# Four graph layers on one core: finer waits on reused memory, and a symmetry proof moved and split

## The chip, the cores and the metric

The kernel runs on one core of a Trainium2 chip. The metric is the device time of one execution in microseconds. The core has five engines with instruction streams of their own: TensorE (PE, with PEld for its weight loads), VectorE (DVE), ScalarE (ACT), GpSimd (POOL) and SyncE (SP). SP, ACT and POOL issue DMA transfers. Each engine takes its instructions in the order in which the program's scheduler put them.

## The reference

`x` is 4096 x 128 and `adj` is 4096 x 4096, symmetric, of zeros and ones with ones on the diagonal. Four layers follow each other, each `x = layernorm(x + layer(x, adj))`:

```python
# layer 0: hyperbolic attention; h from x @ weight.T on the Poincare ball
adj_att = adj * sigmoid((x_tangent @ wl)[:, None] + (x_tangent @ wr)[None, :] + att_b)
support = einsum('ij,ijd->id', adj_att, logmap(h_i, h_j));  out = proj(expmap0(proj(expmap(h, support))))
# layer 1: four heads of 32; masked softmax of q k^T by adj, gated skip connection
# layer 2: relu(D^-1/2 (adj + I) D^-1/2 x @ weight)
# layer 3: H = x W^T + b; softmax over leaky_relu(s_i + r_j) where adj > 0, times H
```

## The kernel before

The program holds two versions. `Fast` runs always; it uses that `adj` is symmetric and of two values, and it collects marks in `odd` that are not zero if this is false. At the end a flag made of the marks decides whether the general version, `Net`, runs the whole again. For these inputs it doesn't. Everything below is about `Fast`.

Rows are cut into 8 stripes of 512 (`NS` = 8, `S` = 512), so `adj` is 8 x 8 blocks of 512 x 512, each held as [128 partitions, 4, 512].

*Layer 0, prologue* (`layer0`, to about 75 us): x is loaded, turned (`HT`), multiplied by the weight, and scaled on the ball (`HA`, lines 446 to 453). PSUM is `ps_t` with 6 banks and `ps_c` with one. Two adjacency blocks (`early`) are loaded ahead.

*Layer 0, pair loop* (`pair_loop`, to 643 us): over the 36 pairs (I, J) with I <= J, each loading one f32 block (`ad`) and doing both sides of the pair. The order of its instructions is written out by hand (`SHARED_ORDER`, `manual_schedule`). Beside it, `narrow` has POOL's queue copy `adj` to a bf16 version in DRAM, `adjb`.

*Proof and tail* (643 to 742 us): `mirror` proves that `adj` is symmetric. For each of the 28 pairs I < J it fetches both blocks of `adjb` (`low`, `up`, SP's queue, three of each in flight), for the 8 diagonal blocks one. TensorE adds, into one PSUM bank `pm`, minus `low` (line 1699) and plus `up` turned (line 1704), with the factor 2^k in the k-th of 12 blocks (`sized`), so that any difference is left as a nonzero number; VectorE reduces each full bank to a mark (line 1709). In the same time the layer's tail on VectorE and ScalarE (lines 533 to 602 and `normalise_tile`) makes the new X, group by group of four tiles.

*Layer 1, prologue* (`layer1`, 742 to 790 us): X is turned into `XT` (line 166), the q and k projections are cut into two parts (`cut`, lines 2217 to 2221), stored to DRAM (`qk`), and fetched back stacked by POOL's queue (`stack`, line 2195) into `KS` and `QS`; then `V` (in `VA`) and `R` (in `Y`). `attention_unshifted` follows, again in a hand-written order: 8 row stripes, each of 32 steps with scores (`ps`, line 2007), exponential (line 2014), mask (line 2016) and sums (`pv`, line 2033). It also copies `adj` into blocks of f32 in DRAM, `adjf`.

*Layers 2 and 3* (`layers23`, from 1603 us): blocks of `adjf` run through a ring of 8 slots in SBUF (`ring`, loads at line 2337), are multiplied by `Y` in two parts (`halves`, lines 2362 to 2382), and looked at for values other than 0 and 1 (line 2346). Small weights (`w`, `br`, `wn`, `ac`) are loaded by SP's queue ahead of the ring's loads. `attend_factored` is layer 3.

Memory comes from tile pools, opened and closed like a stack. In the kernel before, a new pool that lies over the memory of a closed one waits until all of the closed pool's tiles are done with. Outside the hand-written stretches the scheduler orders each engine's instructions by readiness and priority (earlier in the program is higher).

Of the kernel before, what the change touches and what calls it, by code (L numbers as in the profile page):

```python
# [9 lines left out]
F32 = mybir.dt.float32  # L10
# [7 lines left out]
P = 128  # L18
# [7 lines left out]
S = 512  # L26
# [35 lines left out]
class Net:  # L62
# [30 lines left out]

    def copies(self):
        self.adjT = self.dram.tile([self.NS, self.NS, P, 4, S], F32, tag="adjT", name="adjT")

    def pools(self, ctx, adj, big, t, o):

        self.on_scalar = 4
        if adj:  # L100
            self.adjp = ctx.enter_context(self.tc.tile_pool(name="adjp", bufs=adj))
        if big:
            self.ps_big = ctx.enter_context(self.tc.tile_pool(name="ps_big", bufs=big, space=PSUM))
        self.ps_t = ctx.enter_context(self.tc.tile_pool(name="ps_t", bufs=t, space=PSUM))
        self.ps_o = ctx.enter_context(self.tc.tile_pool(name="ps_o", bufs=o, space=PSUM))
# [4 lines left out]
    def whole(self, I, J):  # L110
        return self.adjT[I, J]

# [19 lines left out]
    def load_row(self, vec, name, pool=None):  # L132

        t = (pool or self.const).tile([P, vec.shape[0]], F32, tag=name, name=name)
        self.nc.sync.dma_start(out=t, in_=vec.partition_broadcast(P))
        return t
# [7 lines left out]
    def load_mat(self, mat, name, pool=None):  # L144
        t = (pool or self.const).tile(list(mat.shape), F32, tag=name, name=name)
        self.nc.sync.dma_start(out=t, in_=mat)
# [164 lines left out]
    def layer0(self, x, weight, bias, att_w, att_b):  # L311
# [4 lines left out]
        with ExitStack() as ctx:  # L316
            self.on_scalar = 4
            keep = ctx.enter_context(tc.tile_pool(name="keep0", bufs=1))
            self.cols = ctx.enter_context(tc.tile_pool(name="cols0", bufs=1))
            adp = ctx.enter_context(tc.tile_pool(name="ad0", bufs=2))  # L320
            pre_pools = ctx.enter_context(ExitStack())
            pre = pre_pools.enter_context(tc.tile_pool(name="pre0", bufs=2))
            self.ps_t = pre_pools.enter_context(tc.tile_pool(name="ps_t", bufs=6, space=PSUM))
            one = pre_pools.enter_context(tc.tile_pool(name="one0", bufs=1))
            self.wide = pre_pools.enter_context(tc.tile_pool(name="wide", bufs=1))
            ps_c = pre_pools.enter_context(tc.tile_pool(name="ps_c", bufs=1, space=PSUM))
# [14 lines left out]
            early = {p: self.load_block(adp, 0, p) for p in range(2)}  # L341

# [171 lines left out]
            late = ctx.enter_context(tc.tile_pool(name="late0", bufs=1))  # L514
            rot = ctx.enter_context(tc.tile_pool(name="rot0", bufs=6))
# [92 lines left out]
    def pair_loop(self, HT, HA, dr, rows, adp, early, rows4):  # L608
# [7 lines left out]
        with ExitStack() as ctx:  # L616
            atp = ctx.enter_context(tc.tile_pool(name="at0", bufs=2))
            wtp = ctx.enter_context(tc.tile_pool(name="sg0", bufs=6))
            wk = ctx.enter_context(tc.tile_pool(name="wk0", bufs=2))
            ps_t = ctx.enter_context(tc.tile_pool(name="ps_t0", bufs=2, space=PSUM))  # L620
            ps_z = ctx.enter_context(tc.tile_pool(name="ps_z0", bufs=2, space=PSUM))
            ps_i = ctx.enter_context(tc.tile_pool(name="ps_i0", bufs=1, space=PSUM))
            ps_j = ctx.enter_context(tc.tile_pool(name="ps_j0", bufs=1, space=PSUM))
# [224 lines left out]
    def layer1(self, Wq, bq, Wk, bk, Wv, bv, Ws, bs, Wb, R):  # L848
# [6 lines left out]
        with ExitStack() as ctx:  # L855
            self.on_scalar = 4
            keep = ctx.enter_context(tc.tile_pool(name="keep1", bufs=1))
# [27 lines left out]
            with ExitStack() as pctx:  # L885
                pre = pctx.enter_context(tc.tile_pool(name="pre1", bufs=1))
                rot = pctx.enter_context(tc.tile_pool(name="rot1", bufs=2))
                self.ps_t = pctx.enter_context(tc.tile_pool(name="ps_t", bufs=8, space=PSUM))
# [59 lines left out]
    def attention_unshifted(self, VA, KS, QS, at0, stack, R, wb):  # L948
# [4 lines left out]
        with ExitStack() as ctx:  # L953
            rot = ctx.enter_context(tc.tile_pool(name="rotf", bufs=1))
            natp = ctx.enter_context(tc.tile_pool(name="natf", bufs=2))
            atp = ctx.enter_context(tc.tile_pool(name="atf", bufs=1))
            ep = ctx.enter_context(tc.tile_pool(name="ef", bufs=3))
            ps_s = ctx.enter_context(tc.tile_pool(name="ps_s", bufs=3, space=PSUM))
            ps_v = ctx.enter_context(tc.tile_pool(name="ps_v", bufs=1, space=PSUM))
# [198 lines left out]
    def attention_shifted(self, V, qk, R, wb, spare):  # L1158
# [4 lines left out]
        with ExitStack() as ctx:  # L1163
            self.pools(ctx, 1, 2, 3, 1)
            self.wide = ctx.enter_context(tc.tile_pool(name="wide", bufs=2))
            keep = ctx.enter_context(tc.tile_pool(name="keeps", bufs=1))
            self.cols = ctx.enter_context(tc.tile_pool(name="cols1", bufs=1))
# [12 lines left out]
            work = ctx.enter_context(tc.tile_pool(name="work1", bufs=1))  # L1180
# [98 lines left out]
    def layers23(self, w2, weight, bias, a_s, a_r, out, Y):  # L1279
# [6 lines left out]
        with ExitStack() as ctx:  # L1286
            RING = 8
            ring = ctx.enter_context(tc.tile_pool(name="ring", bufs=1)).tile([P, RING, 4, S], F32, tag="ring", name="ring")
            keep = ctx.enter_context(tc.tile_pool(name="keep3", bufs=1))
# [10 lines left out]
            pre = pctx.enter_context(tc.tile_pool(name="pre3", bufs=1))  # L1300
            rot = pctx.enter_context(tc.tile_pool(name="rot2", bufs=2))
            wp = pctx.enter_context(tc.tile_pool(name="w2", bufs=4))
            ps_b = pctx.enter_context(tc.tile_pool(name="ps_b", bufs=2, space=PSUM))
# [342 lines left out]

class Fast(Net):

    MARKS = 160

# [934 lines left out]
```

## Time and profile before

| What | us |
|---|---|
| time, median of 3 runs (lowest, highest) | 2021.89 (2018.53, 2024.26) |
| time of the profiled execution | 2022.37 |
| its span, first to last instruction | 2020.6 |
| layer 0 prologue, to the first pair's matmul (L1782) | 75.5 |
| last ScalarE instruction of layer 0's tail (L235) ends | 717.3 |
| last mark of the proof (L1709) ends | 742.4 |
| first exponential of attention (L2014) | 790.4 |
| last sums of attention (L2033) end | 1587.5 |
| first ring matmul of layer 2 (L2382) | 1603.4 |

Busy over the whole span: PE 92%, DVE 86%, ACT 65%, POOL 8%. Lines of the profile name the engine, the line of the kernel, the tiles written and read, and durations; a wait `A <- B: t, n, m` says that A stood t us in all, n times, m at the longest, until B was done. In tables by stage each engine has its busy time and the number of its instructions; the columns after the engines are the granted TensorE clock as a share of full speed, the busy share of the DMA engines, and GB/s.

### The profile page before, as it was taken

What the parts mean: (1) busy time and instruction counts of PE and PEld (TensorE: products, weight loads), DVE (VectorE), ACT (ScalarE), POOL (GpSimd) and SP (SyncE); (2) the same over time, 40 slices, a digit from 0 to 9 for tenths busy, and PEclk for the clock granted to TensorE, in tenths of its full rate; (3) what the DMA queues carried; (4) which work ended last, traced back from release to release, by engine and by line L of the source; (5) the groups of instructions that cost most, each with busy time, mean ns of one, the idle gap of its engine ahead of it and who ended that gap; (6) DMA issues with size and microseconds to landing.
All of it is one profiled execution on the core that took longest, in us unless ns stands there. A gap on an engine that the chain in (4) does not pass through costs nothing.

```text
span 2020.6 us, 23440 instructions
## 1 busy us (share of the span) xinstructions
PE 1861.8 (92%) x8406; PEld 997.6 (49%) x8420; DVE 1738.0 (86%) x2741; ACT 1319.2 (65%) x1665; POOL 171.7 (8%) x269
## 2 busy tenths in 40 slices
PE   4789999999998677999999999999999798899997
PEld 4257776667667455333333333333333476644443
DVE  6579999898898846789998999999999888888986
ACT  5589999999997733777878787777877422210000
POOL 2212111121100311200000000000000000000000
PEclk8569999899998997999999999999999899999999
DMA  3488999898934978996767676768656699978882
GB/s 102 49 141 142 156 151 169 144 177 147 156 111 168 373 263 284 259 267 217 236 215 236 211 230 208 239 215 240 211 209 240 238 422 420 421 281 321 295 278 84
DMA packets 167247, 450.86 MB, mean 223 GB/s; under 512 B 13708, under 2 KB 56876, under 8 KB 142544
## 3 DMA queue, kind: packets, MB, share of 16 engines
q1 hardware_dynamic: 112128, 330.94, 45.3%
q0 software_dynamic: 45632, 50.69, 19.8%
q10 hardware_dynamic: 9360, 67.64, 10.4%
q8 instruction: 68, 1.11, 0.2%
q14 instruction: 59, 0.48, 0.1%
HBM read 472.20 MB, written 111.23 MB: 289 GB/s over the span
## 4 chain that ended last, share of the span: by engine, by line
PE 44%; DVE 25%; ACT 15%; DMA 11%; issue 5%; SPq 0%; ACTq 0%; POOL 0%; DVEq 0%; POOLq 0%
PE pv L2033 11%; PE pa L1576 10%; DVE e L2016 9%; PE ps L2007 6%; ACT e L2014 4%; DMA ring<-adjf 4%; PE pz L1782 4%; DMA up<-adjb 3%; PE pi L1866 2%; DVE nat L1998 2%; PE pj L1881 2%; ACT w L1799 2%; ACT s L1822 2%; PE pz L1785 2%; ACT y L1818 1%
## 5 line engine op out<-in xcount | busy, mean ns | idle before, releaser
L2016 DVE SCALAR_TENSOR_TENSOR e<-at,e 128x2048 f32<-128x2048 bf16 x256 | 582.7, 2286 | 78.4 <-ACT e L2014 77.8
L2014 ACT ACTIVATE e<-ps 128x1024 f32<-128x1024 f32 x512 | 493.1, 1024 | 150.0 <-PE ps L2007 122.0
L2033 PE MATMUL pv<-e,VA 128*64 128x512 f32 x2048 | 497.5, 607 | 6.4 <-DVE e L2016 6.1
L2007 PE MATMUL ps<-QS,KS 128*128 128x512 f32 x1024 | 314.4, 425 | 11.1 <-ACT e L2014 10.4
L2007 PEld LDWEIGHTS ps<-QS,KS 128*128 128x128 f32 x1024 | 170.5, 188 | 238.5 <-ACT e L2014 180.2
L2033 PEld LDWEIGHTS pv<-e,VA 128*64 128x64 f32 x2048 | 124.8, 136 | 250.2 <-issue 214.1
L1576 PE MATMUL pa<-w,Y 128*128 128x512 f32 x448 | 195.3, 594 | 0.0
L1782 PE MATMUL pz<-HT 128*128 128x512 f32 x288 | 173.5, 687 | 10.2 <-DVE w L1854 9.1
L1573 DVE SCALAR_TENSOR_TENSOR w<-rho,col,ring 128x512 f32<-128x512 f32 x224 | 162.8, 747 | 22.3 <-PE pa L1576 9.7
L1866 PE MATMUL pi<-HA,w 128*128 128x129 f32 x1152 | 157.5, 286 | 7.3 <-ACT s L1822 5.3
L1866 PEld LDWEIGHTS pi<-HA,w 128*128 128x128 f32 x1152 | 144.0, 199 | 19.1 <-issue 9.3
L2382 PE MATMUL pa<-ring,Y 128*128 128x512 f32 x512 | 133.1, 411 | 11.9 <-DVE ring L2357 10.0
L1576 PEld LDWEIGHTS pa<-w,Y 128*128 128x128 f32 x448 | 83.7, 190 | 106.1 <-issue 79.9
L1989 ACT ACTIVATE nat<-nat 128x2048 f32<-128x2048 f32 x64 | 122.5, 1915 | 4.1 <-DMA nat<-in_adj_dram 4.1
L1791 DVE TENSOR_SCALAR t<-pz 128x512 f32<-128x512 f32 x144 | 93.7, 684 | 30.3 <-PE pz L1785 30.3
L1881 PE MATMUL pj<-HA,w 128*128 128x129 f32 x896 | 117.5, 288 | 2.1 <-DVE X L1895 1.8
L2382 PEld LDWEIGHTS pa<-ring,Y 128*128 128x128 f32 x512 | 95.9, 192 | 42.3 <-DVE ring L2357 12.8
L1881 PEld LDWEIGHTS pj<-HA,w 128*128 128x128 f32 x896 | 109.9, 200 | 9.9 <-issue 7.2
L1854 DVE TENSOR_TENSOR w<-w,ptz 128x512 f32<-128x512 f32 x112 | 73.7, 681 | 23.5 <-PE ptz L1849 23.3
L1799 ACT ACTIVATE w<-di,dr 128x512 f32<-128x512 f32 x144 | 90.6, 708 | 1.9 <-DMA di<-rows 1.9
L2346 DVE SCALAR_TENSOR_TENSOR odd<-ring 128x1024 bf16<-128x1024 f32 x64 | 78.1, 1220 | 12.8 <-DMA ring<-adjf 12.3
L1830 DVE SCALAR_TENSOR_TENSOR t<-t,s 128x2048 f32<-128x2048 f32 x36 | 82.3, 2285 | 6.7 <-ACT s L1822 6.7
(410 smaller groups left out, 2338.5 us busy)
## 6 DMA issues: line engine op xcount, KB each, us to landing
ring<-adjf SPq DMA_DIRECT2D x128, 1024.0 KB, 12.9
nat<-in_adj_dram ACTq DMA_DIRECT2D x64, 1024.0 KB, 6.0
adjf<-in_adj_dram SPq DMA_DIRECT2D x64, 1024.0 KB, 7.4
ad<-in_adj_dram SPq DMA_DIRECT2D x36, 1024.0 KB, 9.2
adjb<-in_adj_dram POOLq DMA_DIRECT2D x64, 512.0 KB, 11.5
at<-adjb SPq DMA_DIRECT2D x63, 512.0 KB, 3.5
low<-adjb SPq DMA_DIRECT2D x36, 512.0 KB, 5.5
up<-adjb SPq DMA_DIRECT2D x28, 512.0 KB, 6.7
```

The costliest lines, as they stand in the source:

```text
L1573: nc.vector.scalar_tensor_tensor(w, rho[:, I * S : (I + 1) * S], col[:, 0, j : j + 1], at[:, jb, :], op0=ALU.max, op1=ALU.mult)
L1576: nc.tensor.matmul(pa, lhsT=F[:, j, :], rhs=w, start=False, stop=(j == NT - 1), skip_group_check=True)
L1782: nc.tensor.matmul(pz, lhsT=HT[:, j * P : (j + 1) * P], rhs=HT[:, I * S : (I + 1) * S], start=True, stop=False)
L1799: nc.scalar.activation(w[:, jb, :], st[p]["d"][k], AF.Sigmoid, bias=dr[:, 4 * J + jb : 4 * J + jb + 1])
L1866: nc.tensor.matmul(row[I, "po"][ib // 2][:, ib % 2, :], lhsT=st[p]["w0"][:, jb, ib * P : (ib + 1) * P], rhs=HA[:, 4 * J + jb, :], start=False,
L1881: nc.tensor.matmul(pj[:, a, :], lhsT=st[p]["w1"][:, ib, jb * P : (jb + 1) * P], rhs=HA[:, 4 * I + ib, :], start=(ib == 0), stop=(ib == 3),)
L1989: nc.scalar.activation(nat, nat, AF.Identity, accum_out=self.deg2[:, k, i : i + 1])
L2007: nc.tensor.matmul(p[:, h, :], lhsT=KS[:, h2 + h, jb * P : (jb + 1) * P], rhs=QS[I % 2][:, h2 + h, :], start=True, stop=True,)
L2014: nc.scalar.activation(e[:, h2 : h2 + 2, :], p, AF.Exp)
L2016: nc.vector.scalar_tensor_tensor(e, at[:, jb % 4, :].unsqueeze(1).to_broadcast([P, NH, S]), 0.0, e, op0=ALU.not_equal, op1=ALU.mult,)
L2033: nc.tensor.matmul(st["po"][h // 2][g : g + 64, :], lhsT=VA[:, o : o + 64], rhs=e[:, h, :], start=(jb == 0), stop=(jb == NT - 1), skip_gro ...
L2382: nc.tensor.matmul(st["pa"], lhsT=halves[k][:, j, :], rhs=at[:, jb, :], start=(I > 0 and j == k == 0), stop=(j == NT - 1 and k == 1), skip ...
```

## The change

`Fast` opens its pools with `reuse_waits="tile"`: a tile that is placed over memory of closed pools waits for the tiles that lay there, no longer for whole pools. `Net` keeps the waits by pool (`waits = "pool"`, `banks = 6`; in `Fast` they are "tile" and 5, and `EARLY` = 8).

The proof becomes `compare(ctx, pairs, natural)` and is split. Its first 8 pairs are compared in layer 0's prologue (`ahead`), from f32 blocks of `adj` itself, whose upper halves are read as bf16 with a step of two elements; their banks are reduced by a ScalarE square with a sum. The rest of the prologue is given higher priority than this comparison. PSUM there: `ps_t` 5 banks, `ps_c` one, the proof two. The other 20 pairs and the diagonal stay behind the pair loop, in pools at the other end of the memory (`side="right"`). These stay open while layer 1's prologue runs, which is given higher priority than they have; its `ps_t` falls from 8 banks to 6 and its `cut` buffers from 7 to 5. The scale tiles take 6 VectorE instructions where they took 25.

In `layers23` the two `halves` get a pool right behind the ring, and the small weights are loaded by POOL's queue.

```diff
+    waits = "pool"
+    banks = 6
+    def pool(self, **kw):
+        return self.tc.tile_pool(reuse_waits=self.waits, **kw)
...
-            keep = ctx.enter_context(tc.tile_pool(name="keep0", bufs=1))
+            keep = ctx.enter_context(self.pool(name="keep0", bufs=1))
...
-            self.ps_t = pre_pools.enter_context(tc.tile_pool(name="ps_t", bufs=6, space=PSUM))
+            self.ps_t = pre_pools.enter_context(self.pool(name="ps_t", bufs=self.banks, space=PSUM))
...
             early = {p: self.load_block(adp, 0, p) for p in range(2)}
+            self.ahead(pre_pools)
...
+    def ahead(self, ctx):
+        rank = self.tc.cur_priority
+        pairs = [(I, J) for I in range(self.NS) for J in range(I + 1, self.NS)][: self.EARLY]
+        self.compare(ctx, pairs, True)
+        ctx.enter_context(self.tc.high_priority(self.tc.cur_priority - rank + 1))
+
     def mirror(self, ctx):
+        NS = self.NS
+        self.proof, self.rank = ExitStack(), self.tc.cur_priority
+        pairs = [(I, J) for I in range(NS) for J in range(I + 1, NS)][self.EARLY :] + [(I, I) for I in range(NS)]
+        self.compare(self.proof, pairs, False)
+
+    def compare(self, ctx, pairs, natural):
+        keep = ctx.enter_context(self.pool(name="mir", bufs=1, side="right"))
+        rot = ctx.enter_context(self.pool(name="mirt", bufs=3, side="right"))
+        ps = ctx.enter_context(self.pool(name="mirp", bufs=2, space=PSUM, side="right"))
...
-        for k in range(K):
-            for m in range(2):
-                nc.vector.tensor_scalar(sized[:, m, k, :], eye, float((-1) ** m * 2**k), None, op0=ALU.mult)
+        nc.vector.tensor_copy(sized[:, 0, 0, :], self.ident)
+        for lo, n, by in ((1, 1, 2.0), (2, 2, 4.0), (4, 4, 16.0), (8, 4, 256.0)):
+            nc.vector.tensor_scalar(sized[:, 0, lo : lo + n, :], sized[:, 0, 0:n, :], by, None, op0=ALU.mult)
+        nc.vector.tensor_scalar(sized[:, 1, :, :], sized[:, 0, :, :], -1.0, None, op0=ALU.mult)
...
+        def fetch(tag, I, J):
+            if natural:
+                t = rot.tile([P, 4, S], F32, tag=tag, name=tag)
+                nc.sync.dma_start(
+                    out=t, in_=self.adj[J * S : (J + 1) * S, I * S : (I + 1) * S].rearrange("(a p) c -> p a c", p=P)
+                )
+                return t.bitcast(BF16)[:, :, 1 : 2 * S : 2]
+            t = rot.tile([P, 4, S], BF16, tag=tag, name=tag)
+            nc.sync.dma_start(out=t, in_=self.adjb[I, J])
+            return t
...
-            if last:
+            if last and natural:
+                nc.scalar.activation(p, p, AF.Square, accum_out=self.mark())
+            elif last:
                 nc.vector.tensor_reduce(self.mark(), p, AX.X, ALU.max, apply_absolute_value=True)
...
             with ExitStack() as pctx:
+                pctx.enter_context(self.proof)
+                pctx.enter_context(tc.high_priority(tc.cur_priority - self.rank + 1))
...
-                self.ps_t = pctx.enter_context(tc.tile_pool(name="ps_t", bufs=8, space=PSUM))
+                self.ps_t = pctx.enter_context(self.pool(name="ps_t", bufs=6, space=PSUM))
...
-                        cut = rot.tile([P, 2, S], F32R, tag="cut", name="cut", bufs=7)
+                        cut = rot.tile([P, 2, S], F32R, tag="cut", name="cut", bufs=5)
...
+            halved = ctx.enter_context(self.pool(name="halved", bufs=1))
+            halves = [halved.tile([P, NT, D], F32R, tag=f"Y{k}", name=f"Y{k}") for k in range(2)]
...
-            halves = [pre.tile([P, NT, D], F32R, tag=f"Y{k}", name=f"Y{k}") for k in range(2)]
...
-            w = self.load_mat(w2, "w2")
-            br = self.load_row(bias, "br3", keep)
-            wn = self.load_mat(weight, "wn3", pre)
+            w = self.load_mat(w2, "w2", queue=nc.gpsimd)
+            br = self.load_row(bias, "br3", keep, nc.gpsimd)
+            wn = self.load_mat(weight, "wn3", pre, nc.gpsimd)
...
-                nc.sync.dma_start(out=ac[:, k : k + 1], in_=v.unsqueeze(1))
+                nc.gpsimd.dma_start(out=ac[:, k : k + 1], in_=v.unsqueeze(1))
```

## The prediction

> **What bounds the kernel now.** I read the slices of the page first, for stages in which no engine is full; then busy time by stage at the places that the change touches; then the waits and the chain there. In the long loops TensorE, VectorE and ScalarE are all near full, so time can only come from the seams between stages. The change touches three: the first layer's prologue (0 to 75.5 us), the step from layer 0 to layer 1 (643 to 790), and the step from attention to layer 2 (1581 to 1603).
>
> Busy time of each engine by stage (length, then PE, PEld, DVE, ACT, POOL; granted clock, DMA share, GB/s):
>
> ```profile
> 31.00:46.00 15.00, 0.00 (x0) 0.00 (x0) 13.67 (x77) 10.07 (x17) 1.04 (x1) 0.53 0.00 1
> 46.00:68.00 22.00, 11.97 (x32) 5.85 (x32) 21.26 (x49) 11.34 (x32) 8.27 (x8) 0.50 0.00 0
> 75.50:108.50 33.00, 32.96 (x37) 9.65 (x38) 9.85 (x13) 22.40 (x15) 6.33 (x10) 0.50 0.62 76
> ...
> 694.00:717.50 23.50, 15.84 (x158) 9.99 (x160) 21.05 (x126) 14.05 (x40) 0.00 (x0) 1.00 0.99 367
> 717.50:742.40 24.90, 17.68 (x190) 12.47 (x191) 2.77 (x4) 0.00 (x0) 0.57 (x1) 1.00 0.74 256
> 742.40:786.00 43.60, 38.65 (x194) 29.49 (x194) 33.43 (x55) 13.05 (x20) 14.02 (x21) 0.84 0.96 322
> ...
> 1581.00:1587.60 6.60, 5.57 (x26) 1.59 (x26) 5.17 (x5) 2.82 (x6) 0.00 (x0) 1.00 0.00 0
> 1587.60:1603.00 15.40, 2.74 (x15) 2.11 (x14) 12.97 (x64) 4.07 (x10) 0.00 (x0) 0.64 0.71 280
> 1603.00:1760.00 157.00, 144.03 (x619) 109.42 (x619) 134.59 (x373) 37.29 (x118) 0.00 (x0) 0.98 1.01 417
> ```
>
> The prologue is VectorE's from 31 to 68 us; the DMA engines do nothing, and TensorE idles at half clock. From 717.5 to 742.4 VectorE works 2.8 us and ScalarE not at all. Layer 2 is bound by its transfers: DMA share 1.01 at 417 GB/s.
>
> The chain of waits through the second seam, and the waits at the second and third:
>
> ```profile
> 719.04 6.28 DMA up<-adjb
> ...
> 734.53 4.50 DMA low<-adjb
> ...
> 742.50 3.69 PE pt L166 x32
> ```
>
> ```profile
> POOL VA L2204 <- PE pm L1704: 54.3, 1, 54.3
> ACT XT L181 <- PE pt L166: 27.6, 1, 27.6
> ```
>
> ```profile
> SPq L2337 <- PE pv L2033: 13.4, 1, 13.4
> ...
> SPq L135 <- DVE X L2107: 10.7, 1, 10.7
> ```
>
> The mirror proof's fetches (low, up) run to 742; layer 0's last ScalarE instruction ends at 717.3. Layer 1's transposes (pt L166) start only when the proof has released its pools. At the third seam the ring's first loads (L2337) wait for the last pv matmul, and the queue then stands behind br (L135), which waits for attention's last normalisation.
>
> **The change, part by part.** (1) *Eight pairs leave the proof after the pair loop.* Its 28 pairs run from the first fetch at 642.9 to 726.9, 3.0 us each (1 MB at 350 GB/s), and its 8 diagonal blocks to 741.4. With 20 pairs the same pace ends at 642.9 + 60 + 14.5 = 717.4, just when the tail ends. That alone is 24 us. The scale tiles there, 24 instructions in 2.46 us before, become 6 over the same columns: 0 to 1.5 us of VectorE; I take 0.
>
> (2) *Layer 1's prologue no longer waits for the proof.* Its transposes can follow each normalised group of X, from 701.5 on. What limits then? VectorE: from 694.0 the tail needs 21.05 - 2.1 (three proof reduces of 0.68) = 19.0 us, layer 1's prologue 33.4 us (16 cuts at 0.74, 16 maxima at 0.67, XT, V and R copies), about four reduces 2.7 us: end at 694 + 55 = 749. Transfers: 20 pairs and 8 diagonals are 25.2 MB, the 16 cut stores 8.4 MB, the 16 stacks needed at once 4.2 MB: 37.8 MB at 375 GB/s is 101 us from 643, end at 744. So VectorE is late next, the transfers hard behind. I add 3 us of gaps: 752, against 785.3 (end of the R copies); the 5.1 us from there to the first attention exponential (790.4) stay. Gain of (1) and (2) together 33 us, of which 24 are (1). Cut buffers fall from 7 to 5: before, 5 of 16 cuts waited for a store (9.9 us); spread between the tail's instructions a cut comes every 2.6 us or so and 5 buffers cover 13 us, about the median landing of 12.6; cost 0, up to 5 if stores land no sooner than that when cuts come at 1.4 us. On SP the cut stores stand behind the proof's fetches, which wait for TensorE to free a slot; by (1) nearly all are through by 710, so I cost this at 0; without that cover each fetch ahead costs 1.5 us. KS and QS lie over layer 0's tiles, so the 16 stacks on POOL (0.55 us each to issue) wait for the tail, but need 9 us of the 30 that are left.
>
> (3) *The ring.* By tile, the ring waits for KS alone, last read by the scores at 1580.9, not for pv at 1587.5; and br, wn, ac leave SP's queue for POOL's. Before, 4 blocks had landed by 1599 and the queue stood still until 1602.7. After: 8 blocks at 2.5 us (1.05 MB at 417 GB/s) land by 1601. TensorE starts near 1603 as before (the ending's VectorE chain sets it) with 4 blocks more in hand, worth 10 us of transfer in a stage bound by transfers. TensorE is busy 144.0 and VectorE 134.6 of the 157 us, so at most 13 us can go. Between 0 and 10 I take 7: VectorE and TensorE become the next bound in single rows. The loads on POOL: POOL is free there, weights needs them at 1609.7, and they can go from about 1588. [...] VectorE is busy 12.97 of 15.4 us there. By the stack rows (0.55 us to issue, 11 to land among full transfers) six loads need some 15 us of the 20; [...]. I take 0, and 5 as the far end. Halves in a pool of their own shift addresses only.
>
> (4) *The prologue.* Sixteen 1 MB fetches on SP, behind early's: 16.8 MB. Before, X and the two ad blocks moved at 290 to 390 GB/s, so 43 to 58 us from 11 us on: through by 54 to 69, before 75.5. If that cover is gone, each us past 75.5 is a us of delay. Behind them on SP stand only later weights and the small rows stores at 75.2. TensorE: 32 blocks of one 512-wide and four 128-wide matmuls. The old proof's steps were 0.22 + 0.22 us at full clock and 0.43 + 0.43 at half: 14 or 27.5 us, against 29.6 idle between 31 and 75.5. The new operands are every second bf16 of an f32 block, which no row shows: at the bf16 rows 14 to 27.5 us, at twice that (the f32 pz pair takes 0.86 us, 0.43 a matmul) 28 to 55, and pairs would start up to 25 us late; [...]. I take the bf16 rows: same operation and shape. ScalarE: 3 squares of 0.69 + 0.19, in its 15 idle us. VectorE: 6 scale instructions in the 9 us that it idles from 11 to 31. Five pt banks instead of six: a group needs one. But engines take instructions in order: HA's transposes (L448) and ScalarE's junk (L446) can stand behind a proof matmul or square whose block is late, and VectorE waits for both. From 0 to 10 us; I take 2.
>
> *The clock.* The pair loop starts at clock 0.50 and keeps it until 134, though PE is busy 32.96 of 33 us; ScalarE idles 9.5 us between 80 and 120 for it. [...] the trace shows 58 us, so a proof that lasts to 75 could bring up to 9.5. But before, the clock fell within 3 us of the last dense matmuls at 31, and by the transfers the proof ends 6 us or more early. I take 0.
>
> Sum: -33 - 7 + 2 = -38. The profiled execution took 2022.4 (span 2020.6 and 1.8 around it), 0.5 above the median of the runs: 2022.4 - 38 - 0.5 = 1984.
>
> **The rivals.** *Only the bytes go.* Tile waits may open nothing, if layer 1's work still stands behind the proof in the engines' orders: then the seam ends 24 us earlier and not 33, and the ring, with its load behind the same kind of order, brings 0 to 7: 1991 to 2000. For: a list order is fixed before the run. Against: 717 to 742 has VectorE and ScalarE empty.
> *A warm start.* Proof fetches stretch to 75 and the clock holds: 9.5 more, 1974. For: between 663 and 742 bursts of proof alone held 1.00. Against: a pair here takes 2 MB, bursts come every 5.6 us and not every 3.
> *The prologue waits for its proof* (slower). The pair loop's matmuls stand behind the last proof matmul in TensorE's order. It decides once the proof ends after 75.5 + 40 = 115 us, that is with fetches under 16.8 MB / 104 us = 162 GB/s, or matmuls of over 2.2 us a block (115 - 31, less 15 of other work, over 32). At 130 GB/s: end at 140, +64 - 40: 2046. For: 13 MB in the first 140 us is all that was ever asked there. Against: 357 to 391 GB/s in the proof's fetches later, 290 to 390 at 10 us.
>
> **How the numbers follow.** Likeliest 0.56 (1975 to 1992); warm start 0.16; only the bytes 0.20; a prologue that gives back nearly all, 0.03; slower 0.05. The time is the likeliest's, 1984. The range runs from a warm start with the whole 10 of the ring, no gaps and no delay (1984 - 9.5 - 3 - 3 - 2 = 1966) to the bytes alone with a prologue 10 us late (2008). A difference of 0.3% (6 us) is about what a measurement of this kernel can tell from none: faster 0.92, same 0.03, slower 0.05.
>
> **What would show it.** Right: first attention exponential 29 to 38 us earlier relative to the pair loop's end; transposes L166 of layer 1 starting near 702 less the shift, between proof matmuls; ring loads issued some 6 us before the last pv without a gap; pair loop starting at 74 to 79. Wrong: VectorE gaps over 10 us between the tail and layer 1's V copies; a first pz after 85; DMA share still 1.01 all through layer 2 with its length unchanged; a clock of 1.00 from 75.

## The result, and the profile after

The changed kernel takes 1990.31 us (median of 4 runs, 1988.17 to 1993.97) against 2023.08 (2018.53 to 2028.32) for the kernel before in the same session: ratio 0.984, 95% interval 0.9816 to 0.9864. Forecast: 1984, range 1966 to 2008. The profiled execution took 1991.43, span 1989.6, so 31.0 less of span where I forecast 38.

Four marks split those 31.0 us. Line numbers are those of the changed kernel from here on.

| stage | before | after | difference | forecast |
|---|---|---|---|---|
| start to the pair loop's last addition into X | 643.6 | 640.0 | -3.6 | +2 |
| from there to the first exponential (the second seam) | 146.8 | 124.8 | -22.0 | -33 |
| first exponential to the end (attention's ending, ring, layers 2 and 3) | 1230.2 | 1224.8 | -5.4 | -7 |

Busy time by stage of the changed kernel, columns as before:

```profile
31.00:46.00 15.00, 9.80 (x91) 7.11 (x93) 10.87 (x57) 10.33 (x16) 1.04 (x1) 0.87 0.98 352
46.00:68.00 22.00, 15.85 (x76) 9.45 (x74) 21.90 (x62) 13.15 (x39) 7.51 (x7) 0.58 0.86 308
75.50:108.50 33.00, 23.88 (x62) 8.88 (x62) 19.23 (x22) 25.50 (x21) 8.56 (x14) 0.82 0.93 138
...
690.00:700.00 10.00, 5.43 (x30) 3.92 (x31) 8.98 (x52) 3.69 (x11) 0.00 (x0) 0.53 0.07 14
...
720.50:761.90 41.40, 33.33 (x162) 22.88 (x160) 30.48 (x49) 11.47 (x17) 10.90 (x20) 0.88 1.02 332
...
1561.60:1577.00 15.40, 12.94 (x65) 9.97 (x63) 14.77 (x64) 5.82 (x10) 0.95 (x2) 1.00 0.90 355
1577.00:1734.00 157.00, 140.14 (x592) 104.97 (x593) 137.84 (x385) 37.35 (x122) 0.00 (x0) 0.98 1.01 421
```

The prologue's DMA engines, idle before, are full at 31 to 46 us, and TensorE, which did nothing there, works 9.8 of the 15 us. The loop's first 33 us have a clock of 0.82 (0.50 before), and ScalarE works 25.5 us there (22.4). The stretch in which VectorE and ScalarE stood before, 717 to 742, is gone. In its place there is a hole at 690 to 700: DMA share 0.07, clock 0.53. Layer 2 starts with its transfers at 0.90 and has 1.01 from 1577 on.

The chain of waits through the second seam, after:

```profile
694.03 0.50 ACT X L244
694.57 0.86 PE pt L175 x2
...
703.85 5.01 DMA low<-adjb
...
719.37 0.33 PE pt L175
719.70 0.88 PE pqk L2255 x2
720.60 0.70 ACT cut L2257
...
728.35 9.41 DMA qk<-cut
...
739.37 11.58 DMA qk<-cut
```

Layer 1's transposes (pt L175) start at 694.6 in the midst of the tail, as forecast. But its first projection (pqk L2255) stands directly behind the last transpose, and so the first cut waits for the last group of X: 720.6. From there to the first exponential at 764.8 it takes 44.2 us, where it took 43.3 before. The waits between 680 and 770 us, and SP's queue (`SPq`) at 675 to 745:

```profile
POOL KS L2233 <- ACT cut L2257: 40.0, 1, 40.0
ACT cut L2257 <- DMA qk<-cut: 15.2, 7, 4.8
...
PEld pt L175 <- ACT X L244: 10.9, 9, 7.5
...
PE pt L175 <- ACT X L244: 8.2, 2, 7.2
```

```profile
686.95 25.45 SPq L1722 DMA_DIRECT2D low<-adjb  x8
722.10 22.93 SPq L2264 DMA_DIRECT2D qk<-cut  x13
```

TensorE stands 7 us for X with the proof's last blocks behind it in its order; their slots stay taken, and the eight diagonal fetches drip out over 25 us. That is the hole at 690.

### The profile page after: what moved, and what is told of

Same layout as the page of the kernel before. It is cut to its first block, busy times and chain, and to the rows that moved or that the text cites. A ratio compares the mean times of both kernels' runs of the same rounds, so it can differ in the third digit from the quotient of the medians.

```text
span 1989.6 us, 23419 instructions
## 1 busy us (share of the span) xinstructions
PE 1843.4 (93%) x8408; PEld 991.9 (50%) x8423; DVE 1737.9 (87%) x2726; ACT 1320.4 (66%) x1671; POOL 174.2 (9%) x275
## 4 chain that ended last, share of the span: by engine, by line
PE 43%; DVE 28%; ACT 17%; DMA 7%; issue 5%; SPq 0%; POOL 0%; ACTq 0%; DVEq 0%; POOLq 0%
PE pv L2071 11%; PE pa L1586 10%; DVE e L2054 9%; PE ps L2045 6%; ACT e L2052 4%; DMA ring<-adjf 3%; PE pj L1919 3%; PE pi L1904 3%; DVE nat L2036 2%; ACT w L1837 2%; PE pz L1820 2%; DVE t L1868 2%; ACT s L1860 2%; ACT nat L2027 1%; PE pa L2441 1%
## 5 line engine op out<-in xcount | busy, mean ns | idle before, releaser
L2052 ACT ACTIVATE e<-ps 128x1024 f32<-128x1024 f32 x512 | 493.2, 1024 | 149.4 <-PE ps L2045 122.0
L1820 PE MATMUL pz<-HT 128*128 128x512 f32 x288 | 160.0, 638 | 18.8 <-DVE w L1892 9.8
L2423 PE MATMUL pa<-ring,Y 128*128 128x512 f32 x512 | 132.3, 409 | 14.5 <-DVE ring L2398 10.0
L2027 ACT ACTIVATE nat<-nat 128x2048 f32<-128x2048 f32 x64 | 122.6, 1915 | 4.9 <-DMA nat<-in_adj_dram 4.9
L2423 PEld LDWEIGHTS pa<-ring,Y 128*128 128x128 f32 x512 | 95.9, 192 | 44.3 <-DVE ring L2398 12.8
```

Source lines behind the costliest of these rows:

```text
L1820: nc.tensor.matmul(pz, lhsT=HT[:, j * P : (j + 1) * P], rhs=HT[:, I * S : (I + 1) * S], start=True, stop=False)
L2027: nc.scalar.activation(nat, nat, AF.Identity, accum_out=self.deg2[:, k, i : i + 1])
L2052: nc.scalar.activation(e[:, h2 : h2 + 2, :], p, AF.Exp)
L2423: nc.tensor.matmul(st["pa"], lhsT=halves[k][:, j, :], rhs=at[:, jb, :], start=(I > 0 and j == k == 0), stop=(j == NT - 1 and k == 1), skip ...
```

## The experiments

The marks of all kernels in us, from one profiled execution each; ratio with its 95% interval against the kernel before beside it.

| kernel | loop ends | second seam | first exponential to the start of the last sums | first exponential to the end | ratio |
|---|---|---|---|---|---|
| before | 643.6 | 146.8 | 796.5 | 1230.2 | 1 |
| changed | 640.0 | 124.8 | 796.3 | 1224.8 | 0.984 (0.9816 to 0.9864) |
| E1 no early pairs | 645.0 | 128.0 | 801.6 | 1228.7 | 0.9918 (0.9889 to 0.9947) |
| E2 waits by pool | 636.1 | 122.6 | 796.7 | 1227.2 | 0.9844 (0.9815 to 0.9873) |
| E3 interleaved | 636.8 | 114.6 | 796.5 | 1221.7 | 0.9762 (0.9736 to 0.9788) |
| E4 no priority | 639.1 | 122.0 | 795.5 | 1222.6 | 0.9818 (0.9795 to 0.9841) |
| E5 proved twice | 637.7 | 129.8 | 803.6 | 1229.3 | 0.9888 (0.9861 to 0.9915) |
| E6 small loads and halves as before | 638.4 | 122.7 | 797.3 | 1227.2 | 0.9825 (0.98 to 0.985) |
| E7 interleaved, waits by pool | 644.5 | 113.4 | 796.3 | 1228.3 | 0.9789 (0.9755 to 0.9824) |
| E8 interleaved, ten pairs | 652.4 | 118.4 | 795.7 | 1220.9 | 0.9827 (0.98 to 0.9854) |
| E9 interleaved, weights on POOL | 640.1 | 115.1 | 795.7 | 1220.7 | 0.9777 (0.9757 to 0.9797) |
| E10 interleaved, no priority | 636.1 | 129.1 | 795.8 | 1218.7 | 0.9844 (0.9817 to 0.9872) |
| E11 three cut buffers | 635.3 | 130.5 | 796.2 | 1222.5 | 0.9848 (0.9825 to 0.9871) |
| E12 interleaved, cuts on ScalarE's queue | 640.2 | 125.5 | 795.8 | 1217.5 | 0.9808 (0.9781 to 0.9836) |

How far single marks can be trusted: the changed kernel and E6 do not differ in the second seam, yet their seams are 124.8 and 122.7. Those with eight early pairs do not differ in the loop, and it ends between 635.3 and 644.5 in them. Behind the first exponential the changed kernel, E3, E4 and E8 to E12 have the same attention and the same layers 2 and 3, and they take 1217.5 to 1224.8. So differences of 2 us in a seam, of 9 in the loop and of 7 in the last stretch are not read from one pair of profiles.

**E1, no early pairs.**

```diff
-    EARLY = 8
+    EARLY = 0
```

> All 28 pairs are proved behind the pair loop again (EARLY = 0), all else as in the changed kernel: waits by tile, ring, loads on POOL. Theory (the eight pairs' bytes are nearly all of the gain at the second seam, and the early proof is also what lifts the clock at the loop's start): granted clock 0.50 from 75 to about 130 as before, pair loop 4 us longer than after; behind it eight more pairs at 2.55 us = 20 us, so from the loop's end to the first attention exponential 125 + 20 = 145 us, and the whole about 1990 + 4 + 20 = 2014 us. Rival (waits by tile open the seam by themselves, since layer 1's work runs beside the proof that is left): the seam stays under 132 us and the whole is under 2002.

2007.0 us. The seam is the rival's: 128.0, under 132 and far from the first theory's 145. The whole is neither's, not 2014 and not under 2002. The 28 pairs do not delay layer 1, they run beside it and on into attention, whose stretch grows by 5.1 us (last proof mark at 787). The pair loop starts at clock 0.50 again, as the first theory has it.

**E5, proved twice.** The early proof stays, and all 28 pairs follow behind the loop.

```diff
-        pairs = [(I, J) for I in range(NS) for J in range(I + 1, NS)][self.EARLY :] + [(I, I) for I in range(NS)]
+        pairs = [(I, J) for I in range(NS) for J in range(I + 1, NS)] + [(I, I) for I in range(NS)]
```

> The eight pairs are proved in the prologue as in the changed kernel, and all 28 are proved behind the pair loop as well: the early proof stays, the bytes behind the loop do not shrink. It separates the two things that EARLY does. Theory (the early proof's matmuls lift the granted clock at the loop's start, the bytes behind are a matter of the seam alone): pair loop 560 to 564 us as in every kernel with the early proof, against 568.1 without it; from the loop's end to the first exponential about 128 us as with EARLY = 0; the whole 4 to 8 us under EARLY = 0's 2007, that is 1999 to 2003 us. Rival (the loop is shorter for another reason than the early proof, so that with the full proof behind it nothing is left): loop 567 to 569 us, the whole 2006 to 2010 us.

2000.56 us, as the first theory has it. E1 and E5 have the same proof behind the loop, and E5 has more work before it; the loop ends at 645.0 and 637.7. First E1, then E5, by stage at the loop's start:

```profile
75.00:100.00 25.00, 24.07 (x31) 7.12 (x29) 6.33 (x10) 14.55 (x14) 6.05 (x10) 0.50 0.83 99
100.00:125.00 25.00, 19.64 (x31) 7.63 (x30) 18.89 (x13) 20.73 (x12) 2.49 (x4) 0.50 0.61 105
125.00:150.00 25.00, 25.00 (x114) 16.71 (x112) 18.70 (x19) 24.55 (x30) 5.12 (x9) 0.79 1.02 158
```

```profile
75.00:100.00 25.00, 21.96 (x62) 8.03 (x62) 11.90 (x18) 18.16 (x15) 8.56 (x14) 0.97 0.93 133
100.00:125.00 25.00, 14.61 (x62) 8.72 (x62) 22.41 (x17) 24.84 (x23) 3.99 (x6) 0.76 0.66 158
125.00:150.00 25.00, 21.08 (x101) 13.77 (x101) 18.14 (x18) 23.05 (x21) 4.50 (x8) 0.86 0.67 119
```

With the proof the clock is 0.97 and then 0.76 where it was 0.50, and ScalarE, which is busy 97% of the time from 150 to 600 us in both, has done 66.0 us of work by 150 us instead of 59.8. That head start of 6.2 us is near the 6.4 between the two medians. The two intervals overlap, and one loop's end scatters by more, so the loops of all kernels are the better evidence. From its first matmul to its end the loop takes 568.1 and 568.2 us in the two kernels without early pairs (before, E1). In ten of the eleven with eight early pairs it takes 559.6 to 565.5. The eleventh, E7, has 569.5 in spite of the same head start, so the gain is not sure in a single execution. From E5 to the changed kernel (0.9888 to 0.984, some 10 us) is what the eight pairs cost behind the loop, with their fetches, matmuls and reductions: 5.0 us in the seam and 7.3 in attention by the marks.

**E2, waits by pool** in all of `Fast`.

```diff
-    waits = "tile"
+    waits = "pool"
```

> Waits by pool again in the whole fast path, the eight pairs still in the prologue. Theory (what the waits by tile brought at the second seam is small, since layer 1's transposes had to wait for the last X groups anyway): proof of 20 pairs and 8 diagonals ends near 640 + 60 + 15 = 715 to 720, layer 1 starts there and takes the 48 us that it took before from its first transposes to the first exponential, so the seam is 125 to 129 us against 124.9; the ring gives back its 5.4 us; the whole 1996 to 2000 us. Rival (the waits by tile are what made the seam shorter): seam 135 us or more, the whole over 2006.

1991.96 us, the same as the changed kernel; the seam is 122.6. The rival falls, and the theory's 1996 to 2000 was a little too much. The stretch to the end is 2.4 us longer where 5.4 were expected: the ring's first load waits for the last sums again (it goes 797.4 us after the first exponential, in the changed kernel 790.4).

**E3, interleaved.** In layer 1's prologue each group of four blocks is turned, copied and projected at once.

```diff
-                self.transposed(X, XT)
...
                 for c in range(NC):
                     s = slice(c * S, (c + 1) * S)
+                    p = self.ps_t.tile([P, 4, P], F32, tag="pt", name="pt")
+                    for k in range(4):
+                        nc.tensor.transpose(p[:, k, :], X[:, 4 * c + k, :], self.ident)
+                    self.evacuate(XT[:, s], p.rearrange("p a b -> p (a b)"))
                     for a, w, bias in ((1, wk, bkc), (0, wq, bqc)):
```

> In layer 1's prologue each group of four blocks is transposed and then projected to q and k at once, in place of all transposes first. Theory (the seam fell short because all transposes stand ahead of all projections in TensorE's order, so that no cut can be made before the last group of X at 720): first cut near 700, and what then ends the seam is VectorE's work or the bytes (both about 745 to 752 by my sum), first exponential 750 to 757 in place of 764.8, the whole 1976 to 1982 us. Rival (the chain of cut stores, the five cut buffers and the stacks needs its 44 us behind the tail whatever the order is): first cut earlier, but first exponential within 3 us of 764.8, more waiting of ACT cut and DVE cut, the whole 1987 to 1991.

1976.04 us: the theory holds, and this version beats both kernels. It is 14 us under the changed kernel, of which the seam has 10.2; the rest lies in stretches whose marks scatter by as much. The seam is 114.6 us, which is 32.2 less than before; my step (2) had 33. Its chain, and one stage of it:

```profile
694.86 0.43 PE pm L1735
695.29 2.87 PE pqk L2258 x4
...
707.33 6.54 DMA low<-adjb
...
721.01 5.70 DMA low<-adjb
...
732.93 1.98 PE pqk L2258 x4
...
751.37 1.87 ACT e L2052 x2
```

```profile
697.00:731.40 34.40, 29.23 (x194) 17.23 (x196) 30.74 (x99) 20.73 (x48) 4.93 (x10) 0.99 0.95 301
```

Projections run from 695 on, VectorE is busy 30.7 of 34.4 us and the DMA share is 0.95: the two limits of my sum, side by side. The hole in the transfers is still there (DMA share 0.22 from 690 to 700).

**E7, the same with waits by pool.** Edit of E2 and E3 together.

> Waits by pool, the eight pairs in the prologue, and in layer 1's prologue each group transposed and projected at once. Theory (waits by tile and the order are two locks on the same door: with waits by pool layer 1 cannot start before the proof ends at about 713, by when X is done, so the order inside it matters little): seam 119 to 123 us, the whole 1986 to 1992 us, while the same order with waits by tile gave 114.6 us and 1976. Rival (the order alone makes the gain, by feeding the cut stores earlier within the prologue itself): seam 112 to 116 us, the whole 1975 to 1980 us.

1983.42 us (1977.5 to 1990.03), seam 113.4. My theory of two locks falls: the seam is that of E3 without any wait by tile. The first cut comes 58.6 us after the loop's end although the last mark of the proof comes at 93.6. What it loses against E3 lies in the loop (644.5) and behind attention (1228.3), not in the seam; the two intervals overlap. So what lets layer 1 run beside the proof is something that E2 and E7 share with the changed kernel: the proof's pools stand at the other end of the memory and stay open. That was not undone by itself.

**E4 and E10, no priority** for layer 1's prologue over the proof, with the changed order (E4) and the interleaved one (E10).

```diff
-                pctx.enter_context(tc.high_priority(tc.cur_priority - self.rank + 1))
```

> Layer 1's prologue no longer has priority over the proof that is left: its transposes stand behind the proof's last blocks in TensorE's order. Theory: TensorE's 7 us of waiting for X at 687 to 694 go, with them the hole of 10 us in the fetches at 690 to 700; the proof's last mark comes near 710 in place of 719, and the tail's last normalisation near 714 in place of 720; cuts still start only after the last group of X: first exponential 0 to 6 us earlier, the whole 1984 to 1990 us. Rival (the hole costs nothing, since transfers have room later): first exponential unchanged or up to 3 us later, because the transposes of all groups now come after the proof, the whole 1990 to 1994.

1987.71 us; seam 122.0, about what E6 has with the priority (122.7). The theory's times came, but not its mechanism. The hole is still there:

```profile
690.00:700.00 10.00, 6.23 (x53) 4.69 (x54) 10.00 (x64) 5.43 (x16) 0.00 (x0) 0.66 0.18 58
```

TensorE still stands 6.7 us for X (7.2 in the changed kernel), and the eight diagonal fetches still take 22.6 us to go out (25.45). The last mark starts at 715.8 in place of 718.4, 1.8 us earlier relative to the loop's end. What the hole costs stays open: no run took it away.

> Interleaved, and layer 1's prologue without priority over the proof that is left. In the interleaved version the proof's last fetches stand in the chain of the seam with 17.5%, and the cuts go ahead of the tail's normalisations on ScalarE (last one 731.4 in place of 720). Theory (the priority is needed: without it the projections queue behind the proof's last blocks, and the cuts start at 712 to 718 as in the version without priority alone): seam 119 to 123 us, the whole 1983 to 1989 us. Rival (the priority only stretches the tail; the proof first and the cuts behind it end sooner): seam 110 to 114 us, the whole 1971 to 1976 us.

1987.88 us, as the theory has it; seam 129.1, longer than either has it. The cuts start 72.0 us after the loop (60.2 in E3), and ScalarE waits 22.3 us for projections that stand behind the proof and the copies:

```profile
ACT cut L2259 <- PE pqk L2257: 22.3, 11, 4.8
```

The interleaving needs the priority: without it the seam is 14.5 us longer than in E3.

**E11, three cut buffers** in the changed kernel (`bufs=5` to `bufs=3`).

> The changed kernel with three cut buffers in place of five (seven before). Its ScalarE waited 15.2 us there for a cut's store to land (9.9 with seven buffers), while the chain from first cut to first exponential grew by 0.9 us only. Theory (the buffers cost little, since the order of the transposes sets the start of the cuts and the bytes their end): chain 44 to 48 us, the whole within 4 us of the changed kernel's 1990. Rival (five buffers are already the bound of that chain, so that a store's 10 to 12 us for three cuts in place of five sets the pace: 16 cuts / 3 x 11 = 59 us): chain 58 to 66 us, the whole 2004 to 2012 us.

1990.85 us. First cut to first exponential is 51.1 us against 44.2, between the two theories, and ScalarE waits for stores longer than with five (24.7 us against 15.2). The whole is no slower: in the profiled execution the loop ended 4.7 us earlier and the last stretch was 2.3 us shorter, both within their scatter. With two buffers less costing 6.9 us here, the 0.9 us that the same chain grew from seven to five is a small price.

```profile
ACT cut L2257 <- DMA qk<-cut: 24.7, 12, 4.2
```

**E6, small loads and halves as before.** `w`, `br`, `wn`, `ac` on SP's queue, `halves` in `pre3`; waits by tile stay.

```diff
-            w = self.load_mat(w2, "w2", queue=nc.gpsimd)
+            w = self.load_mat(w2, "w2")
...
```

> The changed kernel with its small loads for layer 2 (w2, br, wn, ac) on SP's queue again and the halves in the pool where they were, waits by tile kept. Theory (my step 3: the ring's 5.4 us come from an SP queue that no longer stands behind br): the stretch from the first exponential to the end is 1228 to 1230 us again, the whole 1994 to 1997 us. Rival (the changed kernel with waits by pool has its ring loads 7 us later and yet ended only 2.4 us later there; what the ring has in hand is hardly used): the stretch is 1224 to 1227 us, the whole 1989 to 1993 us.

1990.07 us, as the rival has it: the time shows no difference. The marks show 1227.2 to the end against 1224.8; E2, with its loads on POOL but its ring behind pv, has 1227.2 too. In E6 TensorE stands 12.7 us for its first sums, as it did before, and SP stands behind br again:

```profile
PEld pa L2414 <- ACT Y L2402: 12.7, 1, 12.7
```

```profile
SPq L144 <- PE pto L2094: 5.7, 1, 5.7
```

TensorE's first ring matmul comes 813.8 us after the first exponential (800.2 in the changed kernel), and still the end is only 2.4 us later. I read this as a stage that depends on when its transfers run, not on when TensorE starts; one pair of marks does not prove it.

**E8, ten early pairs** in the interleaved version (`EARLY = 10`).

> Interleaved prologue of layer 1 with waits by tile, and ten pairs in the first prologue in place of eight. Two more pairs are 4.2 MB there, 11 us at 385 GB/s: fetches end near 76 in place of 65, so the pair loop starts 2 to 5 us later (78 to 81); behind the loop two pairs less are 5 us of fetches. Theory (the tail of the interleaved version is still bound by the proof's fetches, which stand in its chain with 17.5%): seam 109 to 112 us against 114.6, the clock held to 78, the whole 1971 to 1976 us. Rival (VectorE's work is now the bound of the seam, and the prologue pays for the two pairs): seam within 2 us of 114.6, start 3 to 5 us later, the whole 1977 to 1981 us.

1989.84 us, 14 slower than E3 and beyond both theories. Three views: ScalarE in the changed kernel, then in E8, then SP's queue in E8. `w` is the sigmoid that each pair begins with on ScalarE, and `di` a row that it reads:

```profile
80.98 0.58 ACT L1745 ACTIVATE pm<-pm 128x512 f32<-128x512 f32 x1 [5.12 <-PE pm L1740]
...
83.84 1.28 ACT L1837 ACT_TABLE_LOAD   x1 [2.18 <-DMA di<-rows]
85.14 2.56 ACT L1837 ACTIVATE w<-di,dr 128x512 f32<-128x512 f32 x4
```

```profile
84.84 0.58 ACT L1745 ACTIVATE pm<-pm 128x512 f32<-128x512 f32 x1 [9.84 <-PE pm L1740]
...
86.70 0.58 ACT L1745 ACTIVATE pm<-pm 128x512 f32<-128x512 f32 x1 [1.17 <-PE pm L1740]
...
90.57 1.28 ACT L1837 ACT_TABLE_LOAD   x1 [3.18 <-DMA di<-rows]
91.86 0.72 ACT L1837 ACTIVATE w<-di,dr 128x512 f32<-128x512 f32 x1
```

```profile
81.34 0.33 SPq L155 DMA_DIRECT2D wv<-in_L_gnn_Wv_dram  x1
86.41 0.33 SPq L1781 DMA_DIRECT2D di<-rows  x1
```

The squares of the early proof stand ahead of the pair loop's first `w` on ScalarE: with eight pairs ScalarE waits 5.1 us for the proof's last blocks, with ten 9.8 and 1.2. But the wait that ends last is another. After the last square ScalarE stands 3.18 us more for `di`, and SP held the load of `di` back for 4.9 us, until the proof's matmuls at 86 us were done. So the loop's start hangs on the proof through a load as well. The first `w` is 7.5 us later than in E3 (84.35). By 150 us ScalarE has worked 56.7 us since 75, in E3 67.7, and the loop ends 15.6 us later; where the rest of that was lost stays open. The seam gains nothing from two pairs fewer (118.4). A prologue that waits for its proof, the third rival of my prediction, is real, though not by the path that it names; eight pairs are near its edge.

**E9, layer 1's small loads on POOL's queue** in the interleaved version: the eleven loads of wb, wq, wk, wv, ws and biases get `queue=nc.gpsimd`.

> The interleaved version with layer 1's eleven small loads (wb, wq, wk, wv, ws and the biases) on POOL's queue in place of SP's. In the changed kernel eight of these loads... stand ahead of the pair loop's first load di on SP (issued at 80.0 in place of 76.7), and ScalarE's first w follows di's landing (85.1 in place of 81.4). Theory (the prologue's loss is this queue, not the early proof's matmuls): first w of ScalarE 3 us earlier, 81 to 82.5; the whole 1971 to 1976 us. Rival (the last early proof blocks on TensorE and the square at 80.7 hold the loop anyway): di is issued 3 us earlier, but the first w stays at 84 to 85, the whole 1974 to 1980 us.

1977.33 us, the same as E3: the theory has the first `w`, the rival the time. On SP the loop's first load went out at 80.00 in the changed kernel, behind six weight loads (76.73 before; the expectation's eight are a miscount), and at 79.67 in E3. Here, and then ScalarE's first w:

```profile
75.95 0.35 SPq L1781 DMA_DIRECT2D di<-rows  x1
```

```profile
81.39 2.56 ACT L1837 ACTIVATE w<-di,dr 128x512 f32<-128x512 f32 x4
```

The first `w` is 3.0 us earlier than in E3 (84.35). The first pair's matmul was 1.3 us earlier too (74.6 against 75.9), the rest is the wait for `di` (1.71 us in E3), which is gone: now only the early proof's square stands ahead. But the loop ends at 640.1, no earlier than in E3 (636.8). Where the head start went within the loop stays open, since the loop's end scatters by more.

**E12, the cut stores on ScalarE's queue** in the interleaved version.

```diff
-                        nc.sync.dma_start(out=qk[a, :, :, s].rearrange("k p n -> p k n"), in_=cut.bitcast(F32))
+                        nc.scalar.dma_start(out=qk[a, :, :, s].rearrange("k p n -> p k n"), in_=cut.bitcast(F32))
```

> The interleaved version with the 16 cut stores issued by ScalarE's queue in place of SP's, so that the fetches of the proof's diagonal blocks no longer stand behind cut stores that wait for their cuts (in the interleaved version two such fetches, 6.5 and 5.7 us, lie in the chain of the seam, and the proof's last mark came at 95.5 us after the loop in place of 78). Theory (that queue is what ends the seam next): last fetch of the proof 8 to 15 us earlier, last mark 80 to 86 us after the loop's end, seam 104 to 110 us against 114.6, the whole 1966 to 1972 us. Rival (VectorE and ScalarE are full in the seam, and each store on ScalarE's queue makes ScalarE wait for VectorE's half of the cut): the proof ends earlier, but the seam stays 113 to 118 us, the whole 1974 to 1980 us.

1984.33 us; seam 125.5, 11 us longer than E3, outside both theories. The proof ended earlier (88.8 us after the loop, 95.5 in E3), but ScalarE stood for VectorE's half of the cut before some of the stores, and the tail's last normalisation behind it came 102.2 us after the loop's end (94.6 in E3):

```profile
ACT X L244 <- DVE ms L238: 11.3, 5, 4.7
...
ACT X L244 <- DVE cut L2261: 4.7, 2, 3.3
```

The rival's mechanism is seen, its size was wrong. That the two fetches in E3's chain cost anything is not shown: freed of the cut stores, the proof ended 6.7 us earlier, and the seam was longer.

## Why the prediction was right, and where not

The direction and the range held; 31 to 33 us came where 38 were forecast, and the parts did not have the sizes that I gave them. That the sum lies so near is in part luck: the second seam fell 11 us short, and a clock gain that I had put at nothing made up for some of it. Of my own signs, the first exponential 29 to 38 us earlier relative to the loop's end did not come (22.0), and the clock of 1.00 from 75 us, a sign of being wrong, did.

*Step (2), the second seam: -22.0 for -33. This is the step that failed.* I wrote that the cuts come between the tail's instructions, one every 2.6 us or so, behind transposes that start at 701.5. In the code all eight groups of transposes come before the first projection, so the first cut waited for the last group of X at 720.6. I summed VectorE's work and the bytes as if only these limits counted, and did not read the order within the prologue. With that order changed (E3, E7, E9) the seam is 113.4 to 115.1, within 2 us of my sum's 113.8 (790.4 - 33 - 643.6). In E3 both limits are near at the same time, so the sum was about right for that order; the changed kernel does not reach it.

*Waits by tile at this seam: forecast 9 beyond the bytes, measured none.* E2 equals the changed kernel and E7 equals E3 there. So the 9 us were given to the wrong part of the change.

*Step (1), the eight pairs: I gave them 24 us, for a seam in which layer 1 waits for the proof.* Once layer 1 runs beside the proof they cost only about 10 (E5 against the changed kernel). Running beside it brings the other part: E1 with all pairs behind the loop has already taken 18.8 us off the seam, of which 5.1 come back in attention. The gains are not a sum, since both take away the same wait.

*Cut buffers: 0 taken, up to 5.* The chain from first cut to first exponential grew by 0.9; with three buffers by 6.9 more. *Fetches ahead of the cut stores on SP: 0 taken.* All fetches were out by 712.4, before the first store at 722.1, because the cuts were late. So it was the failed step's delay that covered them.

*Step (3), the ring: -5.4 for -7.* In the eight kernels with the same last stretch the gain is 5.4 to 12.7 us against the one profile before, so 7 was a fair size. Its load went 6.8 us earlier relative to the first exponential, as forecast, and waits for the scores only. With one of the two halves of the change left out, the waits (E2, E7) or the loads on POOL (E6), the stretch takes 1227.2 to 1228.3, longer than in any of the eight, but by only 2.4 us; what each half is worth does not resolve. One sentence was wrong: that TensorE starts near 1603 as before. The first ring matmul came at 1565.1, 12.8 us earlier relative to the first exponential, and little of that arrived: transfers are full, at 1.01, from 1577 to 1734, for the same 157 us as from 1603 before. The loads on POOL, taken at 0 with an estimate of 5 as the far end, held nothing up here: POOL issued five of them from 1559.8 to 1562.6 at 0.54 to 0.58 us each, with VectorE busy 2.58 of these 2.8 us. They landed 5.2 to 9.4 us after their issue, and no matmul waited for them.

*Step (4), the prologue: +2 forecast.* The first matmul came 0.7 us later, but that was a poor mark; ScalarE's first `w` came 3.8 us later (85.14 against 81.37). I had said that behind the fetches on SP stand only later weights and the rows stores. The weights stood ahead of `di`: its load went out 3.3 us later (80.00 against 76.73), 0.7 of it since the rows stores were later and the rest for the six weight loads, and it took 0.5 us longer to land. That is the 3.8 us. The early proof's last square was done by 81.7, before `di` landed, and costs nothing here; in E9, without the weights ahead, it is what the first `w` follows. The operands with a step of two ran near the packed rate in the changed kernel, as I had taken (128 and 512 columns):

```profile
L1740 PE MATMUL pm<-sized,up x128: 217/219/314, 32.9 to 80.7; 128*128 128x128 bf16 x128
L1735 PE MATMUL pm<-low,sized x28: 385/389/634, 32.7 to 80.3; 128*128 128x512 bf16 x28
```

The median is 219 and 389 ns; the proof behind the loop has 219 and 379. But its last blocks ran at 80.7 and not by 69, behind the loop's first matmuls.

*The clock: 0 taken, and it did pay.* It held 1.00 from 70 to 95 us. I had let the proof end 6 us or more before the loop; its blocks ran in TensorE's gaps until 80.7. The gain is some 6 us (E1 against E5), two thirds of the warm start's 9.5, and the later first `w` (83.72 in E5, 82.45 in E1) is already counted in it. That hid part of step (2)'s shortfall. What brings full clock back is not shown. In the changed kernel TensorE worked without a gap from 109.5 us and had 1.00 in the row from 115 to 120. In E3 it was full from 110 to 120 in the same loop at 0.50, and in E1 it was busy 24.07 of 25 us from 75 on and stayed at 0.50.

*The rivals.* "Only the bytes go" forecast 1991 to 2000, and the time is at its edge, the second seam 22.0 us shorter for its 24. Tile waits opened nothing at the second seam, as it has it, and what it named, an order fixed before the run, is the cause, though it is layer 1's own order and not the proof ahead of it. "A warm start" came in part: the clock held, and the fetches had not stretched to 75 for it (the last two went out at 60.4 and 60.9). "The prologue waits for its proof" did not decide at eight pairs. At ten it costs 14 us, with a proof that ends near 87 us and not after the 115 that I had named. I had only TensorE's order in mind; ScalarE's squares and the held-back load of `di` tie the loop to the proof as well.

## What to carry to other kernels

When work is allowed to run beside other work, read the order of its own instructions too: a chain that needs the last piece of its input first gains nothing from starting early (in E3, moving eight groups of transposes took 10 us off the seam and 14 off the whole). Busy time and bytes give a bound, and a bound is reached only if the order lets each piece go when its input is there. Two changes that take away the same wait do not add up, so cost each with the other already in place.

## What the runs showed of the hardware

TensorE was full and stayed at half clock in E1: matmuls of f32 kept it busy without a gap from 80 to 110 us at a granted 0.50. The same loop, entered from the proof's bf16 matmuls at 1.00, kept 1.00 until 95 us in the changed kernel:

```profile
70.00:75.00 5.00, 2.74 (x28) 2.01 (x27) 2.70 (x19) 3.27 (x11) 0.17 (x1) 1.00 0.01 3
...
90.00:95.00 5.00, 5.00 (x11) 1.44 (x9) 0.62 (x2) 4.92 (x4) 0.00 (x0) 1.00 1.43 145
95.00:100.00 5.00, 2.87 (x5) 0.95 (x5) 4.47 (x5) 5.00 (x3) 2.49 (x4) 0.67 1.16 136
100.00:105.00 5.00, 2.25 (x5) 1.22 (x5) 4.63 (x3) 4.94 (x4) 0.00 (x0) 0.50 1.25 184
```

It lost full clock at a gap of TensorE of 2.1 us (95.6 to 97.7), but a gap of 2.2 us at 71.3 us had not cost it. So what decides is not shown. The warm start was worth some 6 us in E5 against E1.

A bf16 operand read with a step of two elements cost TensorE next to nothing in the changed kernel: 219 and 389 ns a matmul of 128 and of 512 columns, 219 and 379 packed.
